# Projecting chunks of a second recurrence ahead of their scans' place, with DRAM as their store

## The chip, the cores and the metric

The kernel runs on one core of a Trainium2 chip. The metric is the device time of one execution in microseconds (us), as the median of the runs. TensorE is called PE here (its weight loads PEld), VectorE DVE, ScalarE ACT, GpSimd POOL and SyncE, which issues the DMAs, SP.

## The reference

The input x has 2 sequences of 4096 tokens with 256 channels. A recurrent layer (RWKV) comes first, then two layers of local attention with a gated feed-forward part. All numbers are float32.

```python
h = layernorm(x)
xr, xk, xv = (h * mix + shifted(h) * (1 - mix) for mix in (time_mix_r, time_mix_k, time_mix_v))
r, k, v = xr @ W_r.T, xk @ W_k.T, xv @ W_v.T
wkv = scan over the 4096 tokens of k, v with decay w = -exp(time_decay)
y = group_norm(sigmoid(r) * wkv)       # statistics over all tokens of a sequence
x1 = x + y @ W_o.T
z = layernorm(x1)
for l in range(2):                     # window 128, 8 heads of 64
    z = z + local_attention(rotary(l2norm(shift_token(z) @ wqkv[l]))) @ wo[l]
    z = z + gated_gelu(layernorm(shift_token(z)) @ w1[l] + b1[l]) @ w2[l] + b2[l]
out = x1 + z
```

The group norm needs the statistics of a whole sequence. So no attention block of a sequence can begin before that sequence's recurrence has ended.

## The kernel before

The work of the first sequence's recurrence (`rec`, nine chunks, seven of 512 and two of 256 tokens) comes first. Then come 32 blocks of 512 tokens: 8 blocks in each of two layers for the first sequence, then the same for the second. Each block is four windows of 128 tokens, so there are 128 windows, numbered n. The second sequence's recurrence (`rec2`, 16 chunks of 256 tokens) is laid among the windows of the first sequence.

A chunk of a recurrence is handled in two parts. The first part, `ahead` (line 717), loads x, normalises it, transposes it (PE) and makes k, v and r by matmuls (`project`, line 693). There are two ways of mixing a token with its predecessor. `split` (line 684) uses two sets of weights, scaled by the mix and by one minus the mix (`wnow` and `wold`); it needs four matmuls for each output where the other needs two, and nothing of DVE. `mixed` (line 666) makes a difference `d` and a mixed input `xm` on DVE and uses the plain weights `wraw`, which lie in the same place as `wold` and are loaded over it. The second part, `scans` (line 737), is three scans on DVE with exponentials on ACT and ends with a DMA of the result to DRAM (`zd`). From there the blocks read it back, scale it by the group norm and multiply it by W_o (`mixed_out`, line 885), which also makes the layer norm by calling `normed` (line 911) for each window; `transpose_x` (line 921) then makes the input of the projections of q, k and v.

The order of the work is made by a planner. Every call on an engine is noted with a row (`plan.at`), a cost (`cost`, line 297) and its dependencies. `order` (line 369) then lists all operations: on each engine, of those that could start first, it takes the one with the lowest row. The lists are fixed when the program is built; on the chip each engine runs its own list in order, and so does SP with its DMAs. The cost of a DMA is 60 ns of SP's time and 2000 ns plus its passage until it has landed (line 365).

The recurrence of the first sequence has rows from -90 on. One chunk of `rec2` (AHEAD = 1, line 35) is projected by `split` at row -0.5. The blocks have their window's number as row. Chunk c of `rec2` is scanned at row n + 0.5, n = 5 + int(c * 50 / 16), and chunk c + 1 is projected at that row by `mixed`. `rec2`'s tiles lie in a piece of memory named `arena`, in slots that are taken in turn (`spot`, line 607), two each for x, k, v, r and the transposed input. `rec` has slots there too, and others in tiles that the blocks use later (`lent`, line 1328): pB, h, hT, sq, t2, qk, x and two in `hm`, the tile of the feed-forward part's hidden values. That tile is first written by `gate` (line 1231) at window 5, right after the first matmuls with w1. So `hm` is free until then.

All instructions have line 517 in the profile (or 511 and 513, for `scaled`), since the planner issues them; the tile names tell them apart. `arena` and `wold` mark the recurrences, `gmv` the group norm, `z` and `wot` the start of a block, `wqkv` with `xT` the projections, `kT` with `qT` the scores, `hT` with `w` the matmuls with w1.

Of the kernel before, what the change touches and what calls it, by code (L numbers as in the profile page):

```python
# [15 lines left out]
P = 128  # L16
# [15 lines left out]
NEG = -1e38  # L32
MASKED = -3e38
R_SLOTS = 50
AHEAD = 1

ARENA = (
    (("m ls aa", 2 * T + 2, 1), ("wnow", 6 * D, 1), ("xT", 2 * T + 2, 2), ("x", 2 * T, 2), ("k v", 2 * T, 1)),
# [20 lines left out]
LEAN = 700  # L59
SLACK = 1.06  # L60
LOAD = 1283
TURN = {"row": 195, "col": 95, "full": 199}
SETS = {AF.Exp: 1, AF.Tanh: 1, AF.Gelu: 2, AF.Ln: 3}
QUADS = 4
# [2 lines left out]
class Place:  # L67


    def __init__(self, size, psum=False):  # L70
        self.size, self.psum = size, psum
        self.reads, self.writes = [], []
        self.real = None
        self.users, self.bank = set(), None
        self.turn, self.first = 0, None
# [101 lines left out]
class Plan:  # L177
# [38 lines left out]

    def dram(self, shape, name):
        place = Place(int(np.prod(shape[1:])))
        place.real = self.dram_pool.tile([P, place.size], F32, tag=name, name=name)
        return self.view(place, 0, shape)  # L220

# [75 lines left out]
    def cost(self, o):  # L297

        views = [*o.outs, *o.ins]
        n = max([v.idx.size for v in views] or [1])  # L300
        psum = any(v.place.psum for v in views)
        inside = sum(v.idx.size == n and not v.place.psum for v in o.ins)
        o.set, o.lock, o.half, o.passes, name, hold = None, False, "full", 0, o.name, None
        if o.eng == "tensor":
            trans = name == "transpose"
            left = o.args[1]
            move = o.args[2] if len(o.args) > 2 else o.args[1]
            cols = max(move.idx.size, left.idx.size) if not trans else P
            o.step = (1 if trans else 2) * (cols / 1.2 + (2 if cols >= 256 else 3))
            if not trans and left.shape[0] <= 64:  # L310
                o.half = "row"
            elif not trans and left.idx.size <= 64:
                o.half = "col"
            if o.half != "full":
                o.step /= 2
            o.time = o.step + 150
        elif o.eng == "vector":
            d = 150 + 1.04 * n
            if name == "tensor_tensor_reduce":
                d = 240 + 1.04 * n  # L320
            elif name == "tensor_tensor_scan":
                d, o.lock = 203 + 2.1 * n, True
            elif name == "scalar_tensor_tensor":
                d, o.lock = 200 + 1.05 * n, inside > 1
            elif name == "tensor_tensor":
                o.lock = inside > 1
            elif name == "tensor_scalar":
                d, o.lock = 155 + (1.27 if psum else 0.98) * n, not psum and n > 16
            elif name == "tensor_copy" and not psum:
                d, o.lock = 230 + 0.45 * n, n > 16  # L330
            elif name == "bn_aggr":
                d = 172
            elif name == "reciprocal":
                d = 147 + 4 * n
            o.step, o.time = max(d - 85, 60), d
        elif o.eng in ("scalar", "either"):
            d = (160 if psum else 195) + 0.83 * n
            if name == "scaled":
                d = 305 + 0.76 * n
            elif name == "activation":  # L340
                o.set = SETS.get(o.args[2])
                if o.args[2] == AF.Identity:
                    d = 365 + 0.87 * n
                elif isinstance(o.kw.get("bias"), View):
                    d += 85
            o.step, o.time = d - 100, d
            if "accum_out" in o.kw:
                o.time = d + 200
        elif o.eng == "gpsimd":
            o.lock = name != "memset"  # L350
            if name == "tensor_tensor":
                d = 430 + 156 * n if ALU.pow in o.args else 140 + 2.22 * n
            elif name == "tensor_scalar":
                d = 230 + 1.12 * n
            else:
                d = (100 if name == "memset" else 187) + 0.98 * n
            o.step, o.time = d, d
            hold = d if n > 64 else 100
        else:
            v = min(views, key=lambda v: v.shape[0] * v.idx.size)  # L360
            size = 4 * v.shape[0] * v.idx.size
            rows = max(v.shape[0] if v.shape[0] > 1 else v.shape[1] for v in views)
            ways = max(k for k in range(1, 17) if rows % k == 0)
            o.passes = size / 170 if ways == 16 else size / (25 * ways)
            o.step, o.time = 60, 2000 + o.passes
        o.hold = hold or o.time


    def order(self):
# [49 lines left out]
        while todo:  # L419
# [25 lines left out]
            for o in g:  # L445
# [21 lines left out]
                o.start = t  # L467
                if e == "sync":
                    dma = max(dma, t) + o.passes
                    o.end = max(t + time, dma + 2000)  # L470
                else:
                    o.end = t + time
                if o.lock and e in lock:
# [47 lines left out]
def kernel(ctx: ExitStack, tc: tile.TileContext, a: dict, out: bass.AP):  # L521
# [62 lines left out]
    class Recurrence:  # L584


        def __init__(self, b, lengths, most, spots):
            self.b, self.most, self.spots = b, most, spots
            self.turns = {}
            self.len = lengths  # L590
            self.off = [sum(lengths[:c]) for c in range(len(lengths))]
            self.n = len(lengths)

            self.stats = tile_of([P, 2, S // 256, 6], "stats", 2)

            self.m, self.ls, self.aa = (
                plan.view(*self.spot(t), [P, 2, most + 1]) for t in ("m", "ls", "aa")
            )
            self.s0 = tile_of([P, 2], "s0", 2)
            self.chunks = [{} for _ in range(self.n)]  # L600
# [65 lines left out]
        def mixed(self, c, j):  # L666

            ch, tr = self.chunks[c], self.len[c]
            if "d" not in ch:
                d = ch["d"] = self.t("d", tr)  # L670
                nc.vector.tensor_tensor(d, ch["xT"][:, :, 1:], ch["xT"][:, :, :tr], ALU.subtract)
            xm = self.t("xm", tr)
            for i in range(2):
                nc.vector.scalar_tensor_tensor(
                    xm[:, i, :],
# [14 lines left out]
                for wt, off in ((wnow, 1), (wold, 0))  # L690
            ]

        def project(self, c, j, how):

            ch, tr = self.chunks[c], self.len[c]
            parts = how(c, j)
            dst = ch[j] = self.t("rkv"[j], tr)
            per = T // tr
            for o0 in range(0, 2, per):
                pm = bank([P, T])  # L700
# [13 lines left out]
                else:  # L714
                    nc.scalar.activation(to, of, AF.Tanh, scale=0.5)

        def ahead(self, c, how):
            row = plan.row
            plan.at(row - 1)
            self.load(c)  # L720
# [1 line left out]
            self.transposed(c)  # L722
            plan.at(row)
            for j in (1, 2, 0):
                self.project(c, j, how)


        def factors(self, y, c):
# [156 lines left out]
    def mixed_out(k):  # L885
# [2 lines left out]
        if l:  # L888
            return
        x, z, g = xs[k], zs[k], groups[b]  # L890
        for h in range(2):
            nc.scalar.activation(
                z[:, h, :], z[:, h, :], AF.Identity, bias=g[:, 1, h : h + 1], scale=g[:, 0, h : h + 1]
            )
        for w0 in range(0, NW, 2):
            py = bank([P, 2, D])
            for w in range(2):
                for h in range(2):
                    nc.tensor.matmul(
                        py[:, w, :],  # L900
                        z[:, h, (w0 + w) * P : (w0 + w + 1) * P],
                        wot[:, h, :],
                        start=(h == 0),
                        stop=(h == 1),
                    )
            nc.vector.tensor_tensor(x[:, w0 : w0 + 2, :], x[:, w0 : w0 + 2, :], py, ALU.add)
        nc.sync.dma_start(out=x1d[b][c], in_=x)
        for w in range(NW):
            normed(x[:, w, :])

    def normed(x):

        st = tile_of([P, 6], "st", 4)
        mv = tile_of([P, 2], "mv", 6)
        nc.vector.bn_stats(st, x)
        nc.vector.bn_aggr(mv, st)
        rs = tile_of([P, 1], "rs", 6)
        rsqrt_of(rs, mv[:, 1:2], 1, LN_EPS, ALU.add)
        nc.vector.tensor_scalar(x, x, mv[:, 0:1], rs, ALU.subtract, ALU.mult)

    def transpose_x(k):

# [4 lines left out]
            nc.gpsimd.memset(xT[:, 1, 0:1], 0.0)  # L927
        else:
            nc.gpsimd.tensor_copy(xT[:, 1, 0:1], xTs[k - 1][:, 1, T : T + 1])
        for i in range(2):  # L930
            pt = bank([P, T])
            for w in range(NW):
# [397 lines left out]
        for t, n in (("pB", 1), ("h", 2), ("hT", 1), ("sq", 1), ("t2", 1), ("qk", 2), ("x", 4))  # L1330
        for i in range(n)
    ]
    lent = [(p, 0) for p in lent] + [(plan.places["hm_0"], i * 2 * T) for i in range((NM - 1) // 2)]
    spots = [{}, {}]
    for b, parts in enumerate(ARENA):
        o = 0
# [6 lines left out]
    for t in "kvrfgeq":  # L1343
        while len(spots[0].setdefault(t, [])) < 2:
            spots[0][t].insert(0, lent.pop())

    plan.at(-101)
    rec = Recurrence(0, [T] * (NB - 1) + [T // 2] * 2, T, spots[0])
# [14 lines left out]
    for j in (1, 2, 0):  # L1363
        rec.project(0, j, rec.split)
    rec2 = Recurrence(1, [TR] * (S // TR), TR, spots[1])
    for c in range(rec.n):
        if c + 1 < rec.n:
            plan.at(-90 + c)
# [8 lines left out]
        plan.hold = None  # L1377
    rec.group_norm()
    for c in range(AHEAD):
        plan.at(-0.5)  # L1380
        rec2.ahead(c, rec2.split)
    plan.at(-0.5)
    nc.sync.dma_start(out=wraw, in_=a["w_rkv"])
    rec2.start()
    plan.at(-1)
    nc.gpsimd.memset(ends, 1.0)
# [13 lines left out]
    for n in range(NN + 6):  # L1400
# [5 lines left out]
        for c in range(rec2.n):  # L1406
            if NW + 1 + int(c * R_SLOTS / rec2.n) == n:
                plan.at(n + 0.5)
                if AHEAD <= c + 1 < rec2.n:
                    rec2.ahead(c + 1, rec2.mixed)  # L1410
                rec2.scans(c)
                if c + 1 == rec2.n:
                    rec2.group_norm()
# [142 lines left out]
```

## Time and profile before

| | us |
|---|---|
| median of 3 runs (lowest, highest) | 3010.59 (3009.65, 3012.26) |
| profiled execution | 3013.12 |
| its span, first to last instruction | 3011.2 |
| PE busy in the span | 2947.5 |
| DVE busy | 2218.2 |
| ACT busy | 2024.9 |
| POOL busy | 1437.8 |
| first DVE instruction on gmv (end of `rec`) | 214.2 |
| first matmul of wqkv | 238.3 |
| first matmul of kT with qT | 260.0 |
| first matmul of hT with w (w1) | 346.8 |
| last DVE instruction on gmv starts (end of `rec2`) | 1355.8 |
| mean granted PE clock | 0.995 |
| DMA: moved, mean rate | 182.50 MB, 61 GB/s |

A profile gives for each engine the time in which it executes, the time between, and what released it (a releaser). Times in a trace are from the span's start. PE's matmuls are pipelined, and their ends are modelled, so they overlap each other in the trace. A float32 matmul is two passes, each with its own weight load; a transpose is one. PEclk is the share of the PE clock that the throttle granted.

### The profile page before, as it was taken

The page shows a single profiled execution, that of the slowest core. Times are in us where ns is not written, and L with a number is a line of the kernel's source. Part 1 is how long each engine was busy: PE and PEld are TensorE (multiplying, and loading weights), DVE is VectorE, ACT ScalarE, POOL GpSimd, SP SyncE. Part 2 cuts the span into 40 slices and gives each one's busy share as a digit, 9 for nine tenths or more (in the row PEclk, how much of TensorE's full clock was granted, in tenths as well). Part 3 has the DMA queues.
Part 4 walks back from the last instruction along what each step waited for, and adds up shares of the span by engine and source line. Part 5 has one row for each costly group of instructions (what it writes and reads, how often), then busy time and mean ns, then how long its engine had stood idle before and what let it go on. Part 6 is the DMA issues. An engine that isn't in the chain of part 4 may idle for free.

```text
span 3011.2 us, 48808 instructions
## 1 busy us (share of the span) xinstructions
PE 2947.5 (98%) x15500; PEld 1912.2 (64%) x15500; DVE 2218.2 (74%) x5077; ACT 2024.9 (67%) x5378; POOL 1437.8 (48%) x1705
## 2 busy tenths in 40 slices
PE   9978999999999999999999999999999999999998
PEld 4456566666666666666666666666666666666665
DVE  7888877888788888787676766667766666667663
ACT  7877786777767777676666566656666666666663
POOL 2226655445445454555544544545444545555550
PEclk9989999999999999999999999999999999999999
DMA  2322112111112121111122221111112121111110
GB/s 83 114 74 95 40 54 64 57 56 54 61 57 69 63 63 59 51 56 53 51 63 81 85 60 59 61 61 60 46 47 75 56 63 57 55 55 54 46 43 24
DMA packets 178314, 182.50 MB, mean 61 GB/s; under 512 B 27044, under 2 KB 147716, under 8 KB 177544
## 3 DMA queue, kind: packets, MB, share of 16 engines
q1 hardware_dynamic: 178056, 179.38, 19.4%
q8 instruction: 123, 2.02, 0.3%
q14 instruction: 135, 1.11, 0.1%
HBM read 79.17 MB, written 33.55 MB: 37 GB/s over the span
## 4 chain that ended last, share of the span: by engine, by line
PE 80%; DVE 9%; ACT 5%; DMA 2%; issue 1%; SPq 1%; POOL 1%; DVEq 0%; POOLq 0%; ACTq 0%
PE bank L517 80%; DVE arena L517 3%; SPq L517 1%; ACT arena L517 1%; DMA h<-x 1%; DVE bank L517 1%; ACT pr L517 1%; ACT L517 1%; DVE nmx L517 1%; DVE sq L517 1%; ACT pr L513 1%; DVE x L517 1%; DVE rn L517 0%; DVE qk L517 0%; DVE pB L517 0%
## 5 line engine op out<-in xcount | busy, mean ns | idle before, releaser
L517 PE MATMUL bank<-wqkv,xT 128*128 128x512 f32 x1536 | 722.0, 597 | 0.4 <-ACT xT L517 0.2
L517 POOL TENSOR_TENSOR t<-qk,tab 128x256 f32<-128x256 f32 x512 | 395.3, 792 | 527.2 <-ACT qk L517 408.1
L517 PE MATMUL bank<-hT,w 128*128 128x512 f32 (+1 forms) x1408 | 644.7, 594 | 0.0
L517 ACT ACTIVATE pr<-bank,nmx 128x129 f32<-128x129 f32 (+1 forms) x1024 | 364.6, 376 | 164.8 <-DVE nmx L517 158.3
L517 PEld LDWEIGHTS bank<-hT,w 128*128 128x128 f32 (+1 forms) x1408 | 258.9, 189 | 269.0 <-issue 247.6
L517 PEld LDWEIGHTS bank<-wqkv,xT 128*128 128x128 f32 x1536 | 268.0, 191 | 229.2 <-issue 219.2
L517 POOL TENSOR_TENSOR rn<-rn,mhalf 128x16 f32<-128x16 f32 x128 | 387.8, 3030 | 8.8
L513 ACT ACTIVATE pr<-pr,sums 128x129 f32<-128x129 f32 (+1 forms) x1004 | 329.4, 413 | 42.7 <-DVE pr L517 41.3
L517 DVE TENSOR_REDUCE rn<-sq 128x16 f32<-128x1024 f32 x128 | 155.6, 1215 | 209.6 <-ACT sq L517 209.6
L517 DVE COPY_PREDICATED bank<-packs,bank 128x254 f32<-128x254 int32 x496 | 186.0, 420 | 151.1 <-PE bank L517 150.7
L517 PE MATMUL bank<-w,hm 128*128 128x256 f32 x1280 | 287.3, 379 | 0.0
L517 PEld LDWEIGHTS bank<-w,hm 128*128 128x128 f32 x1280 | 241.4, 190 | 33.2 <-issue 1.3
L517 PE MATMUL bank<-wo,oT 128*128 128x256 f32 x1024 | 250.3, 387 | 0.0
L517 PE MATMUL bank<-kT,qT 64*128 64x256 f32 (+1 forms) x2048 | 246.1, 380 | 0.0
L517 PEld LDWEIGHTS bank<-wo,oT 128*128 128x128 f32 x1024 | 187.9, 190 | 68.3 <-issue 41.0
L517 ACT COPY qk<-bank 128x512 f32<-128x512 f32 x217 | 126.8, 585 | 151.5 <-PE bank L517 143.8
L517 POOL TENSOR_TENSOR dv<-vr,vt 128x512 f32<-128x512 f32 x124 | 168.7, 1360 | 124.5 <-PE bank L517 108.7
L517 PEld LDWEIGHTS bank<-mats,pr 128*128 128x128 f32 x1148 | 134.0, 135 | 136.7 <-issue 54.0
L517 ACT ACTIVATION_READ_ACCUMULATOR pr<-bank,nmx 128x1 f32 x1024 | 218.6, 214 | 0.0
L517 DVE TENSOR_TENSOR pB<-bank,backs 128x512 f32<-128x512 f32 x248 | 169.7, 684 | 66.4 <-PE bank L517 45.6
L517 PEld LDWEIGHTS bank<-kT,qT 64*128 64x128 f32 x2048 | 190.5, 187 | 31.4 <-issue 6.5
L517 POOL TENSOR_TENSOR tab<-tab,qks 128x256 f32<-128x256 f32 x128 | 119.2, 932 | 183.3 <-DMA tab<-in_c_rot_dram 166.2
(150 smaller groups left out, 5573.8 us busy)
## 6 DMA issues: line engine op xcount, KB each, us to landing
vr<-vt SPq DMA_DIRECT2D x124, 224.0 KB
tab<-in_c_rot_dram SPq DMA_DIRECT2D x128, 128.0 KB
kT<-kT SPq DMA_DIRECT2D x64, 256.0 KB
z<-zd SPq DMA_DIRECT2D x16, 512.0 KB
x<-in_x_dram SPq DMA_DIRECT2D x16, 512.0 KB
x1d<-x SPq DMA_DIRECT2D x16, 512.0 KB
x<-x1d SPq DMA_DIRECT2D x16, 512.0 KB
h<-x SPq DMA_DIRECT2D x128, 64.0 KB
```

The source lines that it names most:

```text
L513: self.nc.scalar.activation(dst, src, AF.Copy, scale=scale)
L517: getattr(getattr(self.nc, o.eng), name)(*args, **kw)
```

## The change

Ten chunks of `rec2` instead of one are projected ahead (AHEAD = 10), at row 4 for the matmuls and row 3 for loading, normalising and transposing, instead of row -0.5. The first three (SPLIT) go by `split`, the next seven by `mixed`, for which `wraw` is loaded between them. Chunks 0 and 1 (INSIDE) stay in their slots. The others' k, v and r are written to slots in `hm` (`far`, three in turn), from there by a DMA each to DRAM (`away`), and read back by `back` at the place where the chunk would have been projected before. `d` and `xm` of these chunks lie in `hm` too, one slot each. The projection of chunks 10 to 15 stays where it was. `hm` is no longer lent to the first recurrence, whose slots move to the other lent tiles.

For the first block, `mixed_out`, `normed` and `transpose_x` go by 128 tokens: eight activations of 128 columns instead of two of 512, four banks with one window each instead of two with two, and the normalised values in a new x tile, so that x1 stays whole in the old one. The other blocks are as before.

In the planner's cost a DMA now takes 370 ns of SP's time, or 580 or 800 between two places in SBUF, instead of 60, and 2500 ns instead of 2000 until it has landed.

```diff
-AHEAD = 1
+AHEAD = 10
+SPLIT = 3
+INSIDE = 2
+LAND = 2500
...
-            o.step, o.time = 60, 2000 + o.passes
+            inner = len(views) == 2 and not any(v.place.outer for v in views)
+            o.step = 370 if not inner else 580 if ways in (1, 16) else 800
+            o.time = LAND + o.passes
...
-                    o.end = max(t + time, dma + 2000)
+                    o.end = max(t + time, dma + LAND)
...
         def mixed(self, c, j):
+            early = "early" if ch.get("early") else ""
             if "d" not in ch:
-                d = ch["d"] = self.t("d", tr)
+                d = ch["d"] = self.t(early + "d", tr)
...
-            xm = self.t("xm", tr)
+            xm = self.t(early + "xm", tr)
...
-        def ahead(self, c, how):
+        def ahead(self, c, how, away=False):
...
             for j in (1, 2, 0):
-                self.project(c, j, how)
+                self.project(c, j, how, ("far", "far", "far") if away else "rkv")
+                if away:
+                    d = self.away[c, j] = plan.dram([P, 2, self.len[c]], f"away_{c}_{j}")
+                    nc.sync.dma_start(out=d, in_=self.chunks[c][j])
+
+        def back(self, c):
+            for j in (1, 2, 0):
+                dst = self.chunks[c][j] = self.t("rkv"[j], self.len[c])
+                nc.sync.dma_start(out=dst, in_=self.away[c, j])
...
+        if k == 0:
+            xs[k] = tile_of([P, NW, D], "x", 4)
+        for w0 in range(0, NW, 1 if k == 0 else 2):
+            ws = range(w0, w0 + (1 if k == 0 else 2))
+            if k == 0 or w0 == 0:
+                cols = slice(w0 * P, (w0 + 1) * P if k == 0 else T)
+                for h in range(2):
+                    nc.scalar.activation(
+                        z[:, h, cols],
...
+            if k == 0:
+                normed(xs[k][:, w0, :], x[:, w0, :])
...
+        if k == 0:
+            for w in range(NW):
+                pt = bank([P, 2, P])
+                for i in range(2):
+                    nc.tensor.transpose(pt[:, i, :], x[:, w, i * P : (i + 1) * P], ident)
+                either(xT[:, :, 1 + w * P : 1 + (w + 1) * P], pt)
+            return
...
-    lent = [(p, 0) for p in lent] + [(plan.places["hm_0"], i * 2 * T) for i in range((NM - 1) // 2)]
+    lent = [(p, 0) for p in lent]
...
+    spare = [(plan.places["hm_0"], i * 2 * TR) for i in range(NM - 1)]
+    spots[1].update(earlyd=spare[:1], earlyxm=spare[1:2], far=spare[2:])
...
     for c in range(AHEAD):
-        plan.at(-0.5)
-        rec2.ahead(c, rec2.split)
+        if c == SPLIT:
+            plan.at(-0.5)
+            nc.sync.dma_start(out=wraw, in_=a["w_rkv"])
+        plan.at(4)
+        rec2.chunks[c]["early"] = True
+        rec2.ahead(c, rec2.split if c < SPLIT else rec2.mixed, c >= INSIDE)
...
                 if AHEAD <= c + 1 < rec2.n:
                     rec2.ahead(c + 1, rec2.mixed)
+                elif INSIDE <= c + 1 < AHEAD:
+                    rec2.back(c + 1)
```

More of the change, by code (lines that the diff above doesn't have):

```diff
@@ L72, in __init__ @@
         self.reads, self.writes = [], []
+        self.outer = False
         self.real = None
@@ L218, in dram @@
         place = Place(int(np.prod(shape[1:])))
+        place.outer = True
         place.real = self.dram_pool.tile([P, place.size], F32, tag=name, name=name)
@@ L588, in __init__ @@
             self.b, self.most, self.spots = b, most, spots
-            self.turns = {}
+            self.turns, self.away = {}, {}
             self.len = lengths
@@ L691, in split, with project @@
             ]
-        def project(self, c, j, how):
+        def project(self, c, j, how, put="rkv"):
             ch, tr = self.chunks[c], self.len[c]
             parts = how(c, j)
-            dst = ch[j] = self.t("rkv"[j], tr)
+            dst = ch[j] = self.t(put[j], tr)
             per = T // tr
@@ L890, in mixed_out @@
         x, z, g = xs[k], zs[k], groups[b]
[L891 to L897, printed above, removed]
+        if k == 0:
[7 more added lines that the diff above has]
+                        z[:, h, cols],
+                        z[:, h, cols],
+                        AF.Identity,
+                        bias=g[:, 1, h : h + 1],
+                        scale=g[:, 0, h : h + 1],
+                    )
+            py = bank([P, len(ws), D])
+            for w in ws:
                 for h in range(2):
                     nc.tensor.matmul(
-                        py[:, w, :],
-                        z[:, h, (w0 + w) * P : (w0 + w + 1) * P],
+                        py[:, w - w0, :],
+                        z[:, h, w * P : (w + 1) * P],
                         wot[:, h, :],
@@ L905, in mixed_out, with normed @@
                     )
-            nc.vector.tensor_tensor(x[:, w0 : w0 + 2, :], x[:, w0 : w0 + 2, :], py, ALU.add)
+            x1 = x[:, w0 : w0 + len(ws), :]
+            nc.vector.tensor_tensor(x1, x1, py, ALU.add)
+            if k == 0:
+                normed(xs[k][:, w0, :], x[:, w0, :])
         nc.sync.dma_start(out=x1d[b][c], in_=x)
-        for w in range(NW):
-            normed(x[:, w, :])
-    def normed(x):
+        if k:
+            for w in range(NW):
+                normed(x[:, w, :])
+    def normed(dst, x=None):
+        x = dst if x is None else x
         st = tile_of([P, 6], "st", 4)
@@ L918, in normed @@
         rsqrt_of(rs, mv[:, 1:2], 1, LN_EPS, ALU.add)
-        nc.vector.tensor_scalar(x, x, mv[:, 0:1], rs, ALU.subtract, ALU.mult)
+        nc.vector.tensor_scalar(dst, x, mv[:, 0:1], rs, ALU.subtract, ALU.mult)
     def transpose_x(k):
@@ L929, in transpose_x @@
             nc.gpsimd.tensor_copy(xT[:, 1, 0:1], xTs[k - 1][:, 1, T : T + 1])
+        if k == 0:
+            for w in range(NW):
+                pt = bank([P, 2, P])
[3 more added lines that the diff above has]
+            return
         for i in range(2):
@@ L1365 @@
     rec2 = Recurrence(1, [TR] * (S // TR), TR, spots[1])
+    rec2.turns = dict.fromkeys(("xT", "x", "k", "v", "r"), 0)
     for c in range(rec.n):
@@ L1379 @@
     for c in range(AHEAD):
-        plan.at(-0.5)
-        rec2.ahead(c, rec2.split)
+        if c == SPLIT:
[4 more added lines that the diff above has]
+        rec2.ahead(c, rec2.split if c < SPLIT else rec2.mixed, c >= INSIDE)
     plan.at(-0.5)
-    nc.sync.dma_start(out=wraw, in_=a["w_rkv"])
+    if AHEAD <= SPLIT:
+        nc.sync.dma_start(out=wraw, in_=a["w_rkv"])
     rec2.start()
```

## The prediction

> **What bounds the kernel now.** I read the page's busy shares and slices first, then a table of the stretches between four marks that the tile views date: 214 us (first DVE instruction on gmv, the end of the first recurrence), 261 (about the first scores), 346.8 (first matmul of w1, tile view of hT), 1392 (end of the second recurrence).
>
> ```profile
> PE 2947.5 (98%) x15500; PEld 1912.2 (64%) x15500; DVE 2218.2 (74%) x5077; ACT 2024.9 (67%) x5378; POOL 1437.8 (48%) x1705
> ...
> PE   9978999999999999999999999999999999999998
> ```
>
> ```profile
> 0.00:175.00 175.00, 166.04 (x448) 80.47 (x448) 139.53 (x260) 139.55 (x237) 45.38 (x88) 1.00 0.26 88
> 175.00:214.00 39.00, 26.24 (x104) 21.44 (x104) 31.84 (x65) 25.05 (x42) 7.07 (x16) 0.87 0.26 81
> 214.00:261.00 47.00, 41.25 (x168) 29.30 (x168) 42.35 (x103) 32.04 (x50) 22.48 (x34) 0.93 0.41 138
> 261.00:347.00 86.00, 76.82 (x469) 51.85 (x466) 70.55 (x176) 62.38 (x197) 60.39 (x70) 0.98 0.18 54
> 347.00:907.00 560.00, 551.11 (x2987) 363.43 (x2986) 451.41 (x1028) 401.30 (x1056) 284.59 (x344) 1.00 0.19 57
> 907.00:1392.00 485.00, 477.48 (x2558) 315.00 (x2557) 401.53 (x882) 355.02 (x937) 245.15 (x274) 1.00 0.19 58
> 1392.00:2810.00 1418.00, 1415.12 (x7783) 925.20 (x7782) 968.59 (x2305) 901.62 (x2559) 702.86 (x807) 1.00 0.20 60
> ```
>
> Columns: stretch, length, busy time of PE, weight loads, DVE, ACT, POOL, then PE's granted clock and the DMA share. From 347 us on PE is idle 19 us out of 2463: there a microsecond of matmul taken away is a microsecond of the end. Between 175 and 347 us PE is idle 28 us of 172 and the clock falls to 0.87 and 0.93, while DVE is 82 to 90% busy. So the change must be read as work moved from a stage that PE bounds into one with holes.
>
> Busy time flatters PE, because each pass's modelled end overlaps the next. The passes' spacing is the true price:
>
> ```profile
> 1504.68 4.48 PE L517 MATMUL bank<-w,hm 128*128 128x256 f32 x20
> 1509.00 1.88 PE L517 MATMUL bank<-hT,w 128*128 128x512 f32 x4
> ...
> 1515.13 3.60 PE L517 MATMUL bank<-hT,w 128*128 128x512 f32 x8
> 1518.57 1.04 PE L517 MATMUL bank<-mats,qk 128*128 128x128 f32 x8
> 1519.44 1.88 PE L517 MATMUL bank<-wqkv,xT 128*128 128x512 f32 x4
> ```
>
> A line's start and count give it: (1509.00 - 1504.68)/20 = 0.216 us for 256 columns, 3.44/8 = 0.43 for 512, 0.87/8 = 0.109 for a transpose. A matmul is two passes, a transpose one. I price the built programs' PE lists so (passes on half the array at half). Before: 2837 us in all, 289.1 ahead of the first w1 matmul, 161.3 of them by 175 us. So 175 to 346.8 holds 127.8 us of matmul and loses 44; from there on 2548.3 us of matmul take 2664.4.
>
> The Trainium skill ("Perfetto Trace Analysis", Identifying the Most-Contended Engine) speaks against reading PE so: matmul busy time is no measure of the distance from the limit, weight loads are. By their 64% PE would not bind, and the 33.5 us of late matmuls that the sum below takes off would save nothing; the back-to-back spacing above contradicts that here.
>
> **Part by part.**
>
> *Late stage, removed.* A chunk projected by `mixed` costs PE 24 passes x 0.216 + 4 transposes x 0.109 = 5.6 us. The order of before has chunks 0 to 2 and a piece of chunk 3 ahead of the first w1 matmul; the changed order has 0 to 9. Rec2's matmuls behind that point fall from 70.7 to 33.6 us: **-37.1**. Other matmuls worth 3.6 move behind it. Net -33.5, all in a stage where PE binds. DVE's mixing of the same chunks leaves the stage with them. PE's idle time in 347 to 1392 is 16 us; I credit **-3** (0 to -10) of it to a DVE that is less full.
>
> *Early stage, added.* Chunks 1 and 2 go by `split`, four matmuls where `mixed` has two: 24 more matmuls, 48 x 0.216 = 10.3 us of PE that did not exist before. Ahead of the first w1 matmul PE now has 333.0 us instead of 289.1; between 175 us and there 333.0 - 161.3 = **171.7**, where before spent 171.8 on 127.8. If every hole were filled, the w1 matmul would come at 346, where it comes now. It can't be that good: the other bound is DVE. Pricing DVE's list from gmv to the first hT eviction at the mean of each like instruction in the trace gives 114 us before and **134** after (42 mixings instead of 16, 0.52 each with their queueing; the first chunk's scans stay, later ones slip). Before needed 131 us for 114, 87%. At 87 to 95% 134 us end at 355 to 368. ACT's list grows from 91 to 103 us and doesn't bind. I take **365**: DVE at 89%, PE at 90%. Bounds: 350 (PE at 98%) and 390 (the same 44 us lost as before).
>
> *First block by 128 tokens.* Now z at 220.4 is followed by the first wqkv matmul at 238.3. For one window the chain is two z activations, two matmuls, one add (0.42), statistics (0.40 + 0.17), POOL (0.23 + 0.72), one scaling (0.41), transposes and one copy (0.58): with handoffs 6 to 8 us, so the projection comes some 10 us sooner. Price: 8 activations for 2; an activation of 128 columns isn't in the trace for z, between 0.38 (pr) and 0.82 (z) each, so +1.5 to +5 us on ACT, of which only the first pair is in the chain. I take 3. That gain is in the 365: without it scores come no sooner than now and the added work is paid in full.
>
> *Half clock.* Before has PE waits of 3.6 us at 178 and 6.3 us at 197 for ACT's arena, and a granted clock of 0.87 and 0.93 in two stretches: 39 x 0.13 + 47 x 0.07 = 8 us lost. PE now has chunks 1 and 2 to do there; these 8 are within the 44, and the 365 takes most of them back. The Trainium skill ("TensorE: Matmul & The Clock Gate", What's actually happening) has the clock halve after an idle window of about 3.4 us; by it all 8 come back if no such gap stays, and none if one does in each place.
>
> *DRAM.* 24 write-outs and 24 read-backs of 256 KB, 12.6 MB on 182. The DMA share is 0.2 to 0.4, so bandwidth isn't it. Each costs SP an issue of 0.3 to 0.6 us (the z loads: 0.335), 48 x 0.45 = 22 us over a queue with room; on the path 0 if their landing is early. A read-back that waits for its arena slot holds up what stands behind it on SP: the vr, h and tab loads. Nearest row: SP waited 45.6 us in 18 times for DVE's arena. Bounds: 0 to 24 x 2.5 us = 60. I take 0: chunk c + 1 is read into the slots of chunk c - 1, whose scans stand a whole chunk ahead.
>
> *wraw* is now loaded behind chunk 2's matmuls, and chunks 3 to 9 wait for it: 768 KB, due while PE does the first block's wqkv. I take 0, to 5 if that cover is short.
>
> *Issue times and landing in the planner's cost.* They change no instruction, only the order everywhere. PE's idle from 347 to 2810 is 19 us: so at most -19, and as much lost if the new order fits worse. I take 0.
>
> **Sum.** First w1 at 365, then 2664.4 - 33.5 - 3 = 2628: a span of **2993** against 3011.2. The profiled execution lay at 3013.1 and the median of the runs at 3010.6, 0.6 below that span: **2992**, 0.6% less.
>
> **Rivals.**
> 1. *DVE is the bound of the early stage (0.20).* It is 90% busy in 214 to 261 already, and the new PE work hangs on its mixing through one xm buffer. At 84 to 78% the 134 us end at 374 to 386, so the span at 3002 to 3014; at 80%, 382 + 2628 = 3010, no change. For it: DVE's figures. Against: the added chunks are independent of the block and can fill any gap.
> 2. *SP's queue stalls (0.12), slower.* Read-backs reach the head before their slot is free, and the shift copies behind them are late for DVE's norms, which PE waits for. Half of the 60 us reaching PE: 2992 + 30 = 3022. It decides from 0.75 us per read-back on (18 us). For it: SP is in order, and it already waits 331 us for DVE's x. Against: PE's own waits name a DMA only for pB (5.5 us).
> 3. *Better (0.18).* PE is kept at 97% early (352), and the late stage sheds 10 us: 352 + 2621 = 2973.
> 4. *Forecast (0.50)*: first w1 between 356 and 375, 2983 to 3002.
> That the chunks aren't ahead at all is excluded by the built order.
>
> **Chances.** Faster by over 0.2% (6 us, about what a measurement of this kernel can tell from no change): all of 4 and 3, and the lowest fifth of 1, 0.50 + 0.18 + 0.04 = 0.72. Within: the rest of 1, 0.16. Slower: 2, 0.12. Range: from rival 3 to the upper end of rival 1, 2973 to 3011; rival 2 is left out.
>
> **What will show it.** First w1 matmul at 356 to 375; DVE near 89% from 214 to there; clock 1.00 from 175 to 261; PE passes on hm with wold between 230 and 365; few PE waits on away loads; 347 to 1392 shorter by 30 to 40 us for the same blocks. Wrong: first w1 beyond 383, or SP waits with PE idle behind them.

## The result and the profile after

| | before | after |
|---|---|---|
| median of 4 runs (lowest to highest), us | 3010.4 (3009.65–3012.26) | 2972.3 (2970.34–2972.81) |
| profiled execution, its span, us | 3013.12, 3011.2 | 2972.24, 2970.5 |
| first matmul of wqkv, us | 238.3 | 225.9 |
| first matmul of kT with qT, us | 260.0 | 245.2 |
| first matmul of w1, us | 346.8 | 362.6 |
| from there to the end of the span, us | 2664.4 | 2607.9 |
| mean granted PE clock | 0.995 | 0.998 |

The changed kernel takes 0.9871 of the time before (95% interval 0.9857 to 0.9886). It is faster, as forecast, but by 38 us where the forecast had 18.6 (3010.6 to 2992), and 2972.3 lies 0.7 us below the range. The page of the changed kernel, rows of busy time and of the 40 slices:

```profile
PE 2944.3 (99%) x15548; PEld 1916.3 (65%) x15548; DVE 2219.5 (75%) x5079; ACT 2016.5 (68%) x5368; POOL 1436.7 (48%) x1705
...
PE   9999999999999999999999999999999999999998
...
PEclk9999999999999999999999999999999999999999
```

PE's slices 3 and 4, which showed 7 and 8 before, are full. The same stretches as in the prediction, with the marks of this kernel (213 and 1354 by PE's first and last matmuls on gmv, 246 about the first scores, 362 the first w1 matmul), in the same columns:

```profile
0.00:175.00 175.00, 166.09 (x444) 80.10 (x445) 139.33 (x262) 138.68 (x236) 44.51 (x86) 1.00 0.26 89
175.00:213.00 38.00, 37.39 (x182) 32.62 (x181) 35.31 (x75) 30.49 (x54) 9.81 (x22) 1.00 0.24 80
213.00:246.00 33.00, 31.99 (x140) 21.96 (x140) 25.56 (x62) 21.80 (x40) 17.00 (x28) 1.00 0.56 196
246.00:362.00 116.00, 112.18 (x646) 82.78 (x644) 106.16 (x264) 81.18 (x227) 72.29 (x97) 0.99 0.33 105
362.00:884.00 522.00, 519.65 (x2842) 337.64 (x2841) 446.15 (x1001) 390.89 (x1037) 272.97 (x327) 1.00 0.24 72
884.00:1354.00 470.00, 468.50 (x2526) 308.82 (x2523) 380.69 (x849) 341.24 (x912) 237.80 (x264) 1.00 0.19 58
1354.00:2769.00 1415.00, 1415.00 (x7791) 926.99 (x7791) 972.02 (x2305) 904.46 (x2562) 708.96 (x808) 1.00 0.20 60
```

Up to 362 us the rows are what the forecast drew: clock 1.00 in 175 to 246, and DVE busy 25.56 + 106.16 of the 149 us from 213 on, 88%. From 362 on they are better than it: PE is idle 2.35 + 1.50 + 0.00 = 3.85 us (length less busy), where the like rows of before gave 8.89 + 7.52 + 2.88 = 19.3.

Idle time doesn't tell all of it, because a pass that starts late behind another's modelled end isn't idle. So each kernel's time is split by the forecast's own price of the matmul passes: **content** is the passes at their closest spacing, **loss** is the rest. "Early" is ahead of the first w1 matmul, "late" behind it.

| | early: time = content + loss | late: time = content + loss |
|---|---|---|
| before | 346.8 = 289.1 + 57.7 | 2664.4 = 2548.3 + 116.1 |
| forecast | 365 = 333.0 + 32 | 2628 = 2514.8 + 113.1 |
| after | 362.6 = 333.0 + 29.6 | 2607.9 = 2514.8 + 93.1 |

The forecast's span was 22.5 us too long: 2.4 of them early, 20.1 late. The content is a count of the matmuls in the built order, so it could hardly miss. What failed is the late loss, and the experiments ask what took 23 us from it.

### The profile page after: what moved, and what is told of

Read it like the earlier page. It is cut to its first block, busy times and chain, and to the rows that moved or that the text cites. A ratio compares the mean times of both kernels' runs of the same rounds, so it can differ in the third digit from the quotient of the medians.

```text
span 2970.5 us, 49027 instructions
## 1 busy us (share of the span) xinstructions
PE 2944.3 (99%) x15548; PEld 1916.3 (65%) x15548; DVE 2219.5 (75%) x5079; ACT 2016.5 (68%) x5368; POOL 1436.7 (48%) x1705
## 4 chain that ended last, share of the span: by engine, by line
PE 89%; DVE 6%; ACT 3%; issue 1%; DMA 0%; POOL 0%; SPq 0%; POOLq 0%; DVEq 0%; ACTq 0%
PE bank L524 89%; DVE arena L524 1%; ACT pr L524 1%; DVE sq L524 1%; ACT pr L520 1%; DVE qk L524 0%; DVE x L524 0%; ACT L524 0%; DVE bank L524 0%; ACT arena L524 0%; DVE hm L524 0%; DVE rn L524 0%; DVE pB L524 0%; DVE nmx L524 0%; DVE h L524 0%
## 5 line engine op out<-in xcount | busy, mean ns | idle before, releaser
L520 ACT ACTIVATE pr<-pr,sums 128x129 f32<-128x129 f32 (+1 forms) x990 | 325.8, 413 | 32.8 <-DVE pr L524 32.5
L524 PE MATMUL bank<-pT,vt 128*64 128x128 f32 x2048 | 203.4, 279 | 0.0
```

The lines of the kernel that those rows point to most:

```text
L520: self.nc.scalar.activation(dst, src, AF.Copy, scale=scale)
L524: getattr(getattr(self.nc, o.eng), name)(*args, **kw)
```

## The experiments

Theory one: the planner's new DMA costs did it. The forecast gave them 0, within ±19. Theory two: with ten chunks gone, DVE has time, and the rest of the stage runs better by itself; the forecast gave that 3 us, up to 10. Every run below was timed against the kernel before on its own chip (medians there 3011.5 to 3013.2 us, against 3010.4 on the changed kernel's); ratios have 95% intervals. So a difference between the changed kernel and a run on another chip is uncertain by some 1 to 3 us.

### The parts, one at a time

**after_oldcosts**: the changed kernel with the planner's costs of before.

```diff
-LAND = 2500
+LAND = 2000
...
-            inner = len(views) == 2 and not any(v.place.outer for v in views)
-            o.step = 370 if not inner else 580 if ways in (1, 16) else 800
-            o.time = LAND + o.passes
+            o.step, o.time = 60, 2000 + o.passes
```

> The changed kernel with the planner's old costs of a DMA (60 ns of the queue, 2000 ns to landing); all else as changed. What is to be explained: behind the first w1 matmul the changed kernel took 2608 us where the forecast had 2628. Theory A, queue costs: the order made with real issue times is what removed PE's waits there. Then this one takes 2992 (2985 to 3000), first w1 matmul still at 360 to 368. Theory B, unloading: the mixing that left the late stage removed the waits. Then 2972 (2966 to 2978).

Measured: 2989.0 us, 0.9924 (0.9909 to 0.9939), 16.7 more than the changed kernel. First w1 matmul at 361.1. Early loss 32.8, late loss 105.3. With no instruction changed, only their order, the late loss is 12.2 larger, and the early one 3.2.

**before_newcosts**: the kernel before with the new costs alone (the diff's three lines on cost, and what they call).

> The kernel before with nothing but the new costs of a DMA in the planner. Theory A, queue costs: 2990 (2983 to 2998), the gain all behind the first w1 matmul. Theory B, unloading: 3010 (3004 to 3016).

Measured: 2990.1 us, 0.9928 (0.9914 to 0.9943): 21.8 us from the cost lines alone. First w1 matmul at 346.5 as before, early loss 55.3, late loss 96.8 against 116.1. So nearly the whole gain lies behind 346 us. Its rows for the three late stretches, same columns:

```profile
347.00:907.00 560.00, 556.68 (x3021) 368.91 (x3020) 460.14 (x1059) 410.08 (x1086) 279.81 (x344) 1.00 0.19 58
907.00:1392.00 485.00, 482.62 (x2632) 320.94 (x2631) 401.33 (x891) 358.79 (x942) 251.53 (x285) 1.00 0.19 58
1392.00:2810.00 1418.00, 1417.92 (x7797) 928.52 (x7796) 973.87 (x2300) 905.17 (x2569) 713.21 (x806) 1.00 0.20 61
```

PE's idle time in them is 3.32 + 2.38 + 0.08 = 5.8 us against 19.3, over the very same stretches, and more matmul passes fit into them (3021 records for 2987 in the first).

What moved can be read from the waits (engine, line, releaser: us in all, times, longest). POOL waits for the rotary table, and DVE's norm (`st`) for the shifted copy `h<-x`. Before:

```profile
POOL tab L517 <- DMA tab<-in_c_rot_dram: 166.2, 58, 6.2
...
DVE st L517 <- DMA h<-x: 68.0, 52, 2.9
```

The kernel before with the new costs:

```profile
POOL tab L522 <- DMA tab<-in_c_rot_dram: 99.5, 36, 7.1
...
DVE st L522 <- DMA h<-x: 14.1, 19, 2.5
```

The changed kernel:

```profile
POOL tab L524 <- DMA tab<-in_c_rot_dram: 95.5, 42, 6.3
...
DVE st L524 <- DMA h<-x: 13.1, 14, 3.3
```

And the changed kernel with the old costs:

```profile
POOL tab L522 <- DMA tab<-in_c_rot_dram: 170.1, 57, 6.2
...
DVE st L522 <- DMA h<-x: 64.4, 55, 2.5
```

Both waits go with the costs and not with the chunks. The reading, which the runs below test: a plan that thinks a copy has landed places its user too early; the user stands at the head of DVE's list and everything behind it stands too. The trace of before, at hand when the forecast was made, has this row, and also SP's own: in the tile views of h and z an issue between two places in SBUF took a median of 586 ns (columns: minimum, median, maximum in ns, first and last start), one from DRAM 335, while the plan charged 60. First h, then z:

```profile
L517 SPq DMA_DIRECT2D h<-x x508: 502/586/1548, 278.5 to 2971.2; - x170
```

```profile
L517 SPq DMA_DIRECT2D z<-zd x16: 320/335/432, 49.6 to 2066.0; - x16
```

**before_block128**: the kernel before with the first block by 128 tokens alone (the diff's `mixed_out`, `normed` and `transpose_x`).

> The kernel before with the first block by 128 tokens alone. Both theories: PE has nothing more to do there, so the chain from z to the first scores is shorter by some 10 us and the first w1 matmul comes at 337 to 343: 3002 (2998 to 3010). If the gain is only had where chunks fill the holes: 3010.

Measured: 3013.1 us, 1.0005 (0.9996 to 1.0015): nothing. The first wqkv matmul does come 8 us sooner (230.4), the first scores 7.5, but the first w1 matmul stands at 346.5. What was gained at the block's head is gone by window 5, and early loss is 57.4 as before.

**ahead_alone**: the ten chunks ahead, with the old costs and the first block by 512 tokens.

> The kernel before with ten chunks ahead and their DRAM store, but the old costs and the first block as it was. The first w1 matmul comes later than in the changed kernel by what the first block's chain is worth, at 366 to 375. Theory A, queue costs: 2998 (2990 to 3008). Theory B, unloading: 2979 (2972 to 2986).

Measured: 2990.3 us, 0.9928 (0.9912 to 0.9945): 21.7 us, about all that the forecast had for the whole change (18.6). First w1 matmul at 365.7, early loss 35.3. Late loss 104.3, 11.8 less than before, where I had credited 3 and at most 10.

So both theories hold in part, and they overlap. Costs alone take 19.3 us of late loss and chunks alone 11.8, which add to 31.1, while the two together take 23.0. Put second, each is worth less: the costs 12.2 behind the chunks (105.3 to 93.1), the chunks with the small blocks 3.7 behind the costs (96.8 to 93.1).

### Which of the two costs, or any new order?

The cost edit has a part for SP's issue time and one for landing. And any change of costs makes a new order everywhere; that could be luck.

**before_step**: before_newcosts with LAND = 2000 (issue times alone). **before_land**: before_newcosts with `o.step = 60` (landing alone).

> The kernel before with the new issue times of a DMA alone (landing stays 2000 ns). A window's four shift copies into h take SP 4 x 0.586 = 2.3 us where the planner reckoned 0.24, an error of 2.1 us; the landing's is 0.5 us. If the error's size decides, most of the 21.8 us come from here: 2994 (2988 to 3000), and DVE's waits of its st statistics for h fall from 68 us to under 30. If landing decides: 3008.

> The kernel before with the longer landing alone (2500 ns; issue stays at 60 ns). If the error's size decides: 3006 (3000 to 3012). If landing decides: 2993.

Measured: before_step 3002.4 us, 0.997 (0.996 to 0.998), late loss 102.7, the wait of `st` for h at 19.1 us; before_land 2992.8, 0.9938 (0.9921 to 0.9954), late loss 101.4, that wait at 39.2. I had tied the gain to the size of the planner's error, and this fails: late, the two are within 1.3 us of each other, and nearly all of the 9.5 us between them is early loss (63.1 and 51.9; 57.7 before), which the new order brought along. The waits aren't the measure of it either: 19.1 and 39.2 for h, and 112.2 and 163.9 for POOL's table, go with the same late loss.

**before_slack105**, **before_slack107**: the kernel before with another figure in its costs, the factor on the three other engines' times (line 60), as a control.

```diff
-SLACK = 1.06
+SLACK = 1.05    # before_slack105; 1.07 in before_slack107
```

> A control: the kernel before with the planner's factor on the engines' durations at 1.05 instead of 1.06, which reorders the lists without telling it more of the DMAs. Queue costs (A): 3010 (3004 to 3018), DVE's waits for h stay at 50 us or more. Any reordering can give it (C): anything from 2988 to 3030.

> The same control at 1.07. Queue costs (A): 3010 (3004 to 3018). Any reordering (C): anything from 2988 to 3030; two controls within 8 us of the kernel before speak against C.

Measured: 3012.6 us, 1.0004 (0.9995 to 1.0014), and 3008.4, 0.9989 (0.998 to 0.9999); late loss 114.7 and 109.8, the wait of `st` for h 64.3 and 65.9. Two other orders of the same work leave the loss nearly where it was, so being new wasn't enough here. They were small edits, though (1% of the engines' times), and only two. They also say how far one order differs from another with no such reason: early loss 58.3 and 61.0 against 57.7, late loss lower by 1 and 6 us.

**before_h_only**, **before_all_but_h**: the new costs for the shifted copies h<-x alone, and for all DMAs but these. If the wait of `st` carries the gain, the first has nearly all and the second little.

```diff
...
+            shift = bool(o.outs) and o.outs[0].place in [self.places.get(t) for t in ("h_0", "h_1")]
+            real = shift    # `not shift` in before_all_but_h
+            o.step = 60 if not real else 370 if not inner else 580 if ways in (1, 16) else 800
+            o.half = LAND if real else 2000
+            o.time = o.half + o.passes
...
```

> The kernel before with the new costs for the shift copies into h alone; every other DMA keeps 60 and 2000 ns. Theory H: DVE standing before its st statistics for a copy that is late (68 us in 52 waits) is how wrong DMA costs reach PE. Then PE's loss behind the first w1 matmul falls from 116 us to 98 to 104 and the time to 2990 to 3000. Theory M: many DMAs are misplaced a little and none carries the gain. Then 3003 to 3010.

> The opposite: new costs for all DMAs but the shift copies into h. Theory H: 3008 (3003 to 3014), DVE's waits for h stay over 50 us. Theory M: 2993 to 3000.

Measured: 2997.0 us both, 0.9951 (0.9936 to 0.9966) and 0.9949 (0.9935 to 0.9964), late loss 100.2 and 100.5, the wait of `st` 43.5 and 48.0. Each half alone gains 16 us, both together 21.8. Neither theory stands: the copies into h aren't needed for most of the gain, and they suffice for most of it. The two halves take 15.9 and 15.6 of late loss where both together take 19.3, so mostly the same. Which waits these are is open.

### How right must the landing be?

**after_land3500**, **after_land2250**: the changed kernel with LAND = 3500 and 2250 for 2500.

> The changed kernel with 3500 ns of landing in the planner's cost instead of 2500, more than the copies take. If the real number is what makes the order good: 2975 or more (2972 to 2990). If a margin goes on helping: 2962 to 2970, which would be faster than both kernels.

> The changed kernel with 2250 ns of landing. 3500 took 2987 and 2500 took 2972; 2000 with 60 ns of issue took 2989. If the optimum is flat about the real time: 2970 to 2976. If each value is a draw of the order: anything from 2968 to 2990.

Measured: 2987.3 us, 0.9917 (0.9902 to 0.9932), for 3500; early loss 35.6, late 102.2. And 2970.2, 0.9859 (0.9844 to 0.9873), for 2250; early 25.9, late 93.4. In the trace of before, from the start of a DMA's issue to its last semaphore update took a median of 1.93 us (h<-x), 2.24 (vr<-vt) and 2.15 (tab). But the plan adds a passage, bytes / 170 in ns for the larger copies, to LAND. At 2000 it already has 2.39 us for the 64 KB copies into h (1.92 measured), 2.77 for tab's 128 KB, and 3.35 for the 224 KB copies of vr (2.67 measured for these alone). So landing wasn't priced too low before: 2250 and 2500 are a margin, and there the time is flat; a further 1000 ns costs 15 us, nearly as much as the whole cost edit gained (16.7). The plan then probably holds users back that could run.

Why does a margin help, then? An estimate from the medians, for the four copies into h of one window, issued one behind the other at 0.54, 0.59, 0.58 and 0.85 us: the last, which lands 1.98 us behind its own issue, has landed some 3.7 us after the first began. The plan of before has 2.75; with LAND = 2500 alone it has 3.25, with the new issue times alone 3.76. The error is in the issue times, and a longer landing covers part of it. No run here has the changed kernel with the new issue times and LAND = 2000, or less. With LAND = 2250 the kernel is the fastest of the study, by 2 us, which is within what an order alone may do.

### The early stage

**ahead_newcosts**: the changed kernel with the first block by 512 tokens, as before.

> The changed kernel with the first block as before (ahead and queue costs without the 128-token pieces). The first block by 128 was worth -1 us beside the chunks with old costs and nothing alone. If its 12 us at the first wqkv matmul are lost again in the windows behind it: 2973 (2970 to 2977), first w1 matmul at 361 to 367 as in the changed kernel. If the real queue costs let it through: 2980.

Measured: 2975.4 us, 0.9879 (0.9864 to 0.9893): the small blocks are worth 3.1 us here by the medians, within what the chips differ by. With the old costs they are worth 1.3 (2990.3 to 2989.0), on the kernel before nothing. The first w1 matmul comes at 364.5 without them and 362.6 with them.

**after_split2**: only two chunks by `split`, the third by `mixed` (SPLIT = 2). That takes 5.2 us of matmul away from PE and gives DVE the mixing of that chunk.

> The changed kernel with two chunks by split instead of three. PE has 12 matmuls, 5.2 us, less; the plain weights are wanted earlier, while PE fills the recurrence's last holes with chunk 2. If PE's content decides: 2967. If chunk 2 then waits for DVE's mixing and the weights: 2972 to 2980, with a PE loss ahead of the first w1 matmul over 30 us.

Measured: 2978.9 us, 0.9886 (0.987 to 0.9903), 6.6 more than the changed kernel, with 5.2 less content. Early loss 36.1 for 29.6, late 98.2 for 93.1. Its rows:

```profile
175.00:213.00 38.00, 32.88 (x161) 28.40 (x159) 36.32 (x78) 29.93 (x53) 9.43 (x22) 1.00 0.28 90
213.00:246.00 33.00, 30.19 (x103) 19.67 (x104) 24.94 (x65) 20.79 (x39) 15.46 (x24) 0.90 0.58 191
```

PE is busy 32.9 us in 175 to 213, not 37.4, and the clock falls to 0.90 behind it. The third chunk's matmuls stood where PE would have been idle while DVE was full (36.3 of 38). They were charged as content, and they cost next to nothing: without them the first w1 matmul comes at 361.4, 1.2 us sooner.

**after_twice**: every write-out to DRAM and every read-back is issued twice, 48 more DMAs.

```diff
+                    for _ in range(2):
-                    nc.sync.dma_start(out=d, in_=self.chunks[c][j])
+                        nc.sync.dma_start(out=d, in_=self.chunks[c][j])
...
+                for _ in range(2):
-                nc.sync.dma_start(out=dst, in_=self.away[c, j])
+                    nc.sync.dma_start(out=dst, in_=self.away[c, j])
```

> The changed kernel with every write-out to DRAM and every read-back done twice, the second behind the first's landing: 48 more DMAs, 12.6 MB more. What the forecast put at nothing is priced so. Hidden: 2973 (2970 to 2977). If SP's queue carries it to PE: 48 x 0.75 us or more, 3008.

Measured: 2980.7 us, 0.9893 (0.9876 to 0.9909): 8.4 us for the second set, with an early loss of 33.7 (4.1 more) and a late one of 98.6 (5.5 more). That is 0.18 us for each DMA added, and part of it may be the new order. So the store isn't quite free, and it is far from the stall of rival 2.

## Why the prediction was right in its direction and wrong in its size

- **Bound.** Right. PE's weight loads went from 64% to 65% while its idle time behind 362 us went to 3.85 us; the spacing told the distance from the limit, and the busy share of the weight loads didn't.
- **Late stage, removed: -33.5.** Right, as the count of the built order (2548.3 to 2514.8). In after_oldcosts, where the order's costs are those of before, the time behind the first w1 matmul is 2985.8 - 361.1 = 2624.7, 3.3 below the forecast's 2628; that it is so near is partly luck, as 4.6 us more of matmul fall behind the mark there and the loss is 7.8 smaller than forecast.
- **"I credit -3 (0 to -10)" for a DVE that is less full.** Mis-sized with the costs of before: ahead_alone's late loss fell by 11.8, after_oldcosts' by 10.8. Behind the new costs only 3.7 was left for it.
- **Early stage: first w1 at 365.** Right: 362.6, DVE at 88% (89 forecast), loss 29.6 (32 forecast). In the forecast's case and not in rival 1's or rival 3's.
- **"24 more matmuls … 10.3 us of PE that did not exist before".** They exist, but after_split2 shows a third chunk's share of them to be nearly free; the bound by DVE at 89% had that in it already.
- **First block by 128.** The projection came 12.4 us sooner (some 10 forecast). Of "without it scores come no sooner than now and the added work is paid in full" the first half held (ahead_newcosts has them at 260.0, as before) and the second failed: the w1 matmul comes at 364.5 and the kernel gains 37 us all the same (3012.4 to 2975.4). What fills the early stage is the chunks, not the earlier scores.
- **Half clock.** Right: the waits of up to 6.3 us for ACT's arena are gone, and the clock is 1.00 from 175 to 246. PE's own waits in 100 to 400 us, before and after:

```profile
PE bank L517 <- ACT arena L517: 12.0, 6, 6.3
```

```profile
PE bank L524 <- DVE hm L524: 2.3, 2, 2.2
...
PE bank L524 <- ACT arena L524: 0.7, 2, 0.4
```

- **DRAM: 0 of 0 to 60.** About right, by after_twice under 9 us. PE's own waits in the changed kernel name no DMA at all, neither a read-back nor the load of `wraw`.
- **Issue times and landing: "at most -19, and as much lost if the new order fits worse. I take 0."** This is the step that failed. Late, the costs took 12.2 us off the changed kernel's loss (after_oldcosts) and 19.3 off the kernel before; in the medians 16.7 and 21.8. I took the correction of a known error for a coin toss. The trace showed the sign: SP's issues at 586 ns where the plan had 60, and 68.0 us of DVE waiting for copies that the plan thought landed. That a longer landing would help as well (18.7 us alone, in before_land) was not to be read from the landings, which the plan had long enough. The bound of 19 was too tight, since it counted idle time alone: in before_newcosts the idle time fell by 13.5 us and the late loss by 19.3.

The sum's miss of 20.0 us in the late loss is those two steps. How it divides depends on which comes first: 7.8 of the stall (10.8 for 3) and then 12.2 of the costs, or 19.3 of the costs and then 0.7 of the stall (3.7 for 3, the small blocks with it). Either way the costs, taken at 0, are the larger part. Rival 3 (2973) had the time nearly right by luck, with another sum: 352 + 2621, where 362.6 + 2607.9 was measured. Its 2973 is a span besides, which the range took over as a time without the 0.6 off; and the range's upper end, 3011, isn't the 3014 of rival 1.

What stands of the late loss has a bottom. Of the 23.0 us gained, 20.4 lie ahead of window 60 (loss 64.4 before, 44.0 after); from there to window 120, marked by their w1 matmuls, before, before_newcosts and after all lose 36 to 38 us. In the timeline of the changed kernel (start, us, then the group) the bottom is to be seen:

```profile
1713.22 0.39 PE L524 MATMUL bank<-pB,dv 128*64 128x128 f32 x4
1713.54 0.70 PE L524 MATMUL bank<-w,ends 64*128 64x256 f32 x4
1714.08 1.89 PE L524 MATMUL bank<-kT,qT 64*128 64x256 f32 x16
1715.90 1.99 PE L524 MATMUL bank<-wo,oT 128*128 128x256 f32 x8
1717.73 1.04 PE L524 MATMUL bank<-mats,h 128*128 128x128 f32 x8
```

Four passes of pB at 0.0545 us end at 1713.44; the next group, on another part of the array (64*128 for 128*64), starts at 1713.54. Its own four passes, 0.43 us at 0.108 each, take 0.54, though kT behind it has the same shape. Sixteen passes of kT end at 1715.81, and wo, on the whole array, starts at 1715.90; its eight, 1.73 us at 0.216, take 1.83. So where the shape of the array in use changes, PE loses about 0.1 us at the turn and about as much in the first passes behind it, with nothing waited for. The Trainium skill ("TensorEngine Tiling (Array Packing)", Key Properties) says that a change of tiling mode drains TensorE; the rows agree and give the price. Taken by the medians of each kind over all turns behind the first w1 matmul, three per window, it is 0.55 us per window and 70 us in all, the same in before, before_newcosts and after. So of the late loss 46 us before and 23 after are of another kind. It fits that the gains overlap: little is left to take. No run here changed the turns.

## What to carry to other kernels

When an order is computed from costs, compare each cost with the median in the trace, the issuing engine's own time for a DMA too, and look for engines that wait for what was under-priced: correcting it was more here than a new draw. A margin elsewhere can cover part of such an error, as 500 ns of landing did here, but it has no measured value to stop at: 1 us more cost 15 us. Work moved into a stage with holes should be judged by that stage's second engine, and matmuls that spare that engine can be nearly free there.

## What the runs showed of the hardware

- An issue on SP took, in the medians of before, 0.33 to 0.35 us to or from DRAM for z, x1d and tab, and 0.54 to 0.59 between two places in SBUF for the copies into h and vr, but 0.85 for those of them over 15 partitions.
- The granted clock halved only at steps of a grid of 3.41 us (in the trace of before from 178.5, 195.6, 216.0, 332.1 and 1240.0), and by how long PE was idle within the step just before. In the 17 traces here, from 20 us on, every step at full clock with over 2.0 us of idle PE was followed by half clock; the least that was had 1.78, the most that was not 1.97. The length of one stretch doesn't decide: 2.46 us until 330.9 before (half clock from 332.1) and 2.16 until 253.3 after (from 253.3) were followed by it, 3.13 us until 299.9 before, which lay across two steps, was not. The Trainium skill ("TensorE: Matmul & The Clock Gate", What's actually happening) has the clock halve after an idle window of about 3.4 us; here a step need not be idle throughout.
